# Layer norms and half of the kept-edge evictions of batches 1 to 3: from ACT to DVE, in a quantile-aggregation graph layer

## The chip, the core and the metric

The kernel runs on one core of a Trainium2 chip. The metric is device time in microseconds (us) of one execution, lower being better. A core has a matrix engine (PE), a vector engine (DVE), an activation engine (ACT), GpSimd (POOL) and a synchronisation engine (SP) whose queue issues most plain DMAs here. Each works through its own list of instructions in order; they meet through semaphores.

## The reference

The input is `x` (16 batches of 1024 nodes, 64 values each), a symmetric 0/1 adjacency `adj` (16 x 1024 x 1024, about 8 neighbours a node, with self loops) and a mask that is all ones. Cut to what matters:

```python
h = jnp.maximum(_layernorm(x, axis=-1), 0.0)
# inside the layer, on h, with T, K = 10, 2:
neigh = (adj_ > 0) & ~eye
rank  = jnp.cumsum(ni, axis=-1) - ni            # place of an edge in its row
skip  = jnp.where(nb > T, (nb + K - 1) // K, 1) # nb: neighbours of the node
rem   = neigh & (sk > 1) & (rank % sk == sk - 1) & mask[:, :, None]
rem   = rem | jnp.swapaxes(rem, 1, 2)
nd    = jnp.where(rem, 0.0, adj_) > 0           # edges that are kept
# quantiles 0.25, 0.5, 0.75 of h over the kept neighbours, weighted 0.25, 0.5, 0.25
agg   = sum of w * (v_lo + frac * (v_hi - v_lo))
out   = h + agg
y     = relu(out @ W1 + b1) @ W2 + b2
return x + y * mask
```

So rows with more than 10 neighbours drop a few edges; for each node and each of 64 channels the values at the remaining neighbours are sorted, and three quantiles of them are added to the node's own value before a small two-layer perceptron.

## The kernel before, in words

A batch passes through these stages, each a generator (a Python function that emits instructions and yields) inside `list_layer`:

- `load(b)` (L892): eight adjacency tiles of 128 rows come in by SP's DMAs (`ask`, L813, two buffers). ACT makes 0/1 values of each (L904), PE transposes them (L911), and ACT writes the result as fp8 (L924). `number` (L934) counts the neighbours; its counts go to `cnt`.
- `drop(b)` (L970): PE computes ranks into PSUM, ACT takes a distance (L991), DVE marks dropped edges in `rem` (L992).
- `normalize(b)` (L1198): the layer norm and ReLU. SP loads `x` of the batch into `xt` (L1200, a single buffer). For batch 0 DVE does it in eight whole-tile instructions around one square root on ACT (L1205 to L1213). For the others `scaled` (L1177) does it on ACT in pieces of 64 columns: eight sums (L1181) and eight sums of squares (L1186), each of them two instructions since the accumulator is read out, then eight normalised ReLUs (L1194). L1219 and L1220 copy the values into `pack`; L1231 stores `h` to a table in DRAM, from which the gathers read.
- `keep(b)` (L995): PE subtracts dropped edges in both directions in two PSUM halves for each of eight tiles (L1004 to L1009). The halves are clamped at zero and written to `kept` as fp8: by ACT (L1014), except that for batch 0 DVE writes the second half of each tile (L1012). PE then makes bit codes of the kept edges (L1017), ACT copies them to `pack` (L1022).
- `order(b)` (L1025): nodes are ranked by their number of edges, and DVE builds a permutation matrix `perm` (L1063). `rem` and `perm` share one buffer (the tag "wide"), so `drop` of the next batch can only begin to write when this batch's `perm` has been read.
- `collect(b)` (L1067): PE permutes codes and values (L1088), ACT copies out the values (L1093 to L1098), DVE extracts the neighbour indices (L1103 to L1132). The last of them, L1132, writes the index list `idx`. With it the batch's gathers can begin.

`prepare(b)` (L1629) emits `drop(b)`, `load(b+1)` and `normalize(b)` interleaved, then `keep`, `order` and `collect`.

Batches are used in pairs. `fetch(m)` (L1253) queues the gathers of pair m: 63 for each batch, in four classes of node tiles, all of them indirect DMAs issued by POOL (L1265). The buffers of the first two classes are double, those of the last two single. `aggregate` (L1350) sorts the gathered values with compare-exchange networks of DVE minimum and maximum (L1300, L1305), weighs them (L1316), sums them on PE (L1320); `mlp` (L1448) ends the work on a batch. The main loop (L1678) weaves aggregation and perceptron of pair m-1 with the preparation of pair m+1.

The order in which each engine runs its instructions is not that of emission. `arrange` (L641) takes all instructions with their dependences, prices each (`Step.cost`, L614), and simulates a list schedule: an engine that is free takes, among the instructions that are ready in the model, the one that was emitted first. The resulting sequence of each engine is then fixed by added dependences. On the chip an engine that meets an instruction whose data is not there waits, even if a later one could run.

In `keep` and `normalize` the choice of the engine is made by the batch number; these are the conditions that the change touches:

```python
if b == 0 and n:          # keep, L1011: second half of each tile
    nc.vector.tensor_scalar(kept[:, 4:], kp, 0.0, None, OP.max, saturate=False)
...
if b == 0:                # normalize, L1203
```

Of the kernel before, what the change touches and what calls it, by code (L numbers as in the profile page):

```python
# [547 lines left out]
            main(b, iter(()))  # L548


ENGINES = ("PE", "ACT", "DVE", "POOL", "SP")
NAMES = {"PE": "PE", "DVE": "DVE", "Activation": "ACT", "Pool": "POOL", "SP": "SP"}

# [87 lines left out]
def arrange(tc, runs, loose, tails):  # L641
# [59 lines left out]

    free, wire = dict.fromkeys(ENGINES, 0.0), 0.0
    waiting, able, sequence = ({e: [] for e in ENGINES} for _ in range(3))
# [49 lines left out]
def list_layer(  # L753
# [138 lines left out]
    def load(b, fast=False):  # L892

        ne = wk.tile([P, NT, N], FP8, name="ne", bufs=2)
        neT[b] = ne
        nbs[b] = [wk.tile([P, NT], F32, name=n) for n in ("bias", "half")]
        for t in range(NT):
            ask(b, t)
            at = asked.pop((b, t))
            sg = wk.tile([P, N], BF16, name="sg")  # L900
            if fast and t % 2:
                nc.gpsimd.tensor_scalar(sg, at, 0.0, None, OP.is_gt)
            else:
                nc.scalar.activation(sg, at, AF.Sign)  # L904
            ask(*divmod(b * NT + t + 2, NT))
            for n in range(2):
                tp = psum.tile([P, 4, P], F32, name="tp", tag="mx", bufs=3)
                run = []
                for s in range(4):
                    m = 4 * n + s  # L910
                    run.append(nc.tensor.matmul(  # L911
                        tp[:, s], sg[:, m * P:(m + 1) * P], ident16, start=(s == 0), stop=(s == 3 and t // 4 != n),
                        skip_group_check=True,
                    ))
                if t // 4 == n:
                    run.append(
                        nc.tensor.matmul(tp[:, t % 4], minus16, ident16, start=False, stop=True, skip_group_check=True)  # L917
                    )
                settle(run)
                to = ne[:, 4 * n:4 * n + 4, t * P:(t + 1) * P]  # L920
                if fast and n:
                    nc.vector.tensor_scalar(to, tp, 0.0, None, OP.max, saturate=False)
                else:
                    nc.scalar.activation(to, tp, AF.Relu, saturate=False)  # L924
            if fast and t == 3:
                number(b, 0, 4)
            yield 0.1
        if fast:
            number(b, 4, NT)
        else:  # L930
            number(b, 0, NT)
        yield 1.4

    def number(b, lo, hi):  # L934

        ne = neT[b]
        bias, half = (k[:, lo:hi] for k in nbs[b])
        for n in range(lo // 4, hi // 4):
            cols = slice(n * HALF, (n + 1) * HALF)

            cp = psum.tile([P, HALF], F32, name="cp", tag="mx", bufs=3)
            run = []
            for k in range(2):
                for q in range(4):
                    run.append(nc.tensor.matmul(
                        cp[32 * q:32 * q + 32], one[:, 1 - k:33 - k], ne[:, 2 * q + k, cols], start=(k == 0),
                        stop=(k == 1), skip_group_check=True,
                    ))
            settle(run)
            if b == 0 and n:  # L950
                nc.vector.tensor_copy(cnt[:, cols], cp)
            else:
                nc.scalar.copy(cnt[:, cols], cp)
        nb = psum.tile([P, NT], F32, name="nb", tag="misc")
        settle([
            nc.tensor.matmul(nb[:, t:t + 1], cnt[:, t * P:(t + 1) * P], ones16[:, 0:1], start=True, stop=True)
            for t in range(lo, hi)
        ])
        nb = nb[:, lo:hi]

        sk = wk.tile([P, NT], I32, name="sk")[:, lo:hi]
        nc.vector.tensor_scalar(sk, nb, 1.0, None, OP.add)
        many = wk.tile([P, NT], F32, name="many")[:, lo:hi]
        nc.vector.scalar_tensor_tensor(many, nb, 10.0, mask[:, b, lo:hi], OP.is_gt, OP.mult)
        nc.vector.tensor_scalar(sk, sk, 1, None, OP.logical_shift_right)
        nc.vector.tensor_scalar(bias, sk, -1.5, -2047.0, OP.mult, OP.add)
        nc.vector.tensor_scalar(half, sk, 0.5, 1.0, OP.mult, OP.add)
        nc.vector.tensor_tensor(half, half, many, OP.mult)
# [26 lines left out]
    def keep(b):  # L995

        ne, rem = neT.pop(b), rems.pop(b)
        for t in range(NT):
            ts = slice(t * P, (t + 1) * P)
            kept = wk.tile([P, NT, P], FP8, name="kept")  # L1000
            for n in range(2):
                kp = psum.tile([P, 4, P], F32, name="kp", tag="mx", bufs=3)
                run = [
                    nc.tensor.matmul(kp, plus, ne[:, 4 * n:4 * n + 4, ts], start=True, stop=False),  # L1004
                    nc.tensor.matmul(kp, minus, rem[:, 4 * n:4 * n + 4, ts], start=False, stop=False),  # L1005
                ]
                for s in range(4):
                    at = (4 * n + s) * P
                    run.append(nc.tensor.matmul(kp[:, s], rem[:, t, at:at + P], minus, start=False, stop=(s == 3)))  # L1009
                settle(run)  # L1010
                if b == 0 and n:  # L1011
                    nc.vector.tensor_scalar(kept[:, 4:], kp, 0.0, None, OP.max, saturate=False)  # L1012
                else:
                    nc.scalar.activation(kept[:, 4 * n:4 * n + 4], kp, AF.Relu, saturate=False)  # L1014
            code = psum.tile([P, NT, 17], F32, name="code", tag="code", bufs=2)
            settle([
                nc.tensor.matmul(  # L1017
                    code[:, s], kept[:, s], octet, start=(s == 0), stop=(s == NT - 1), skip_group_check=True
                )
                for s in range(NT)  # L1020
            ])
            nc.scalar.copy(pack[:, t, :KEYS], code.rearrange("p s k -> p (s k)"))  # L1022
            yield 0.1
# [174 lines left out]
    def normalize(b):  # L1198
        xt = wk.tile([P, NT, C], F32, name="xt", bufs=1)
        nc.sync.dma_start(out=xt, in_=x[b].rearrange("(t p) c -> p t c", p=P))  # L1200
        h = xt
        mean, var = (wk.tile([P, NT], F32, name=n) for n in ("mean", "var"))
        if b == 0:  # L1203
            shape, square = [P, NT, C], wk.tile([P, NT, C], F32, name="square", tag="highs", bufs=1)
            nc.vector.tensor_reduce(mean, xt, AX.X, OP.add)  # L1205
            nc.vector.tensor_scalar(mean, mean, -1.0 / C, None, OP.mult)
            nc.vector.tensor_tensor(h, xt, mean[:, :, None].to_broadcast(shape), OP.add)
            nc.vector.tensor_tensor(square, h, h, OP.mult)
            nc.vector.tensor_reduce(var, square, AX.X, OP.add)
            nc.scalar.activation(var, var, AF.Sqrt, bias=eps, scale=1.0 / C)  # L1210
            nc.vector.reciprocal(var, var)
            nc.vector.tensor_tensor(h, h, var[:, :, None].to_broadcast(shape), OP.mult)
            nc.vector.tensor_scalar(h, h, 0.0, None, OP.max)  # L1213
            yield 0.4
        else:
            yield from scaled(xt, mean, var)

        halves, bytes_ = (h.rearrange("p t c -> p (t c)").bitcast(d).rearrange("p (t c k) -> p t c k", t=NT, c=C) for d in (BF16, U8))
        nc.scalar.copy(pack[:, :, VALUES:VALUES + C], halves[:, :, :, 1])  # L1219
        nc.scalar.copy(  # L1220
            pack[:, :, VALUES + C:].rearrange("p t (c k) -> p t c k", k=2), bytes_[:, :, :, 0:2]
        )
        nc.scalar.copy(pack[:, :, OWN + 2], mask[:, b])
        grp, at = divmod(b, GROUP)
        for g in range(B // GROUP) if b == 0 else ():
            group_tab[g] = dram.tile([GROUP, FRONT + N, C], F32, name="gtab", bufs=B // GROUP)
            nc.sync.dma_start(
                out=group_tab[g][:, 0:FRONT].rearrange("b n c -> b (n c)").rearrange("b (s k) -> b s k", s=SLICE),
                in_=none,
            )  # L1230
        nc.sync.dma_start(out=group_tab[grp][at, FRONT:].rearrange("(t p) c -> p t c", p=P), in_=h)  # L1231
        tables[b] = group_tab[grp].rearrange("b n c -> (b n) c")[:(at + 1) * (FRONT + N)], at * (FRONT + N) * C
        yield 0.1
# [641 lines left out]
```

## Time and profile before

| | |
|---|---|
| median of 3 runs | 1548.63 us (1544.91 to 1550.77) |
| the profiled execution | 1547.62 us |
| its span, first to last instruction | 1545.8 us |
| instructions | 28097 |
| mean granted PE clock | 0.84 of full speed |
| ACT busy | 915.4 us (59%) |
| gathers on POOL | 1008, mean 1.05 us each |
| index lists ready (L1132), batches 0 to 5 | 68.4 and 77.2 (two parts), 149.1, 210.8, 273.8, 343.4, 401.7 us |
| first and last gather begin | 68.9 and 1487.5 us |

The profile is one execution. An engine's busy share is an average over stages that have different limits; what ended each idle time, and when, is read from the timeline. A record's duration runs from its start to its end in the engine's pipeline, and records of one engine overlap, so that a sum of durations can be larger than the time that the engine needed. In groups, the columns are: line, engine, operation, tiles, shapes, count, then busy us and mean ns of one, then idle time before them and what ended it.

### The profile page before, as it was taken

The page shows a single profiled execution, that of the slowest core. Times are in us where ns is not written, and L with a number is a line of the kernel's source. Part 1 is how long each engine was busy: PE and PEld are TensorE (multiplying, and loading weights), DVE is VectorE, ACT ScalarE, POOL GpSimd, SP SyncE. Part 2 cuts the span into 40 slices and gives each one's busy share as a digit, 9 for nine tenths or more (in the row PEclk, how much of TensorE's full clock was granted, in tenths as well). Part 3 has the DMA queues.
Part 4 walks back from the last instruction along what each step waited for, and adds up shares of the span by engine and source line. Part 5 has one row for each costly group of instructions (what it writes and reads, how often), then busy time and mean ns, then how long its engine had stood idle before and what let it go on. Part 6 is the DMA issues. An engine that isn't in the chain of part 4 may idle for free.

```text
span 1545.8 us, 28097 instructions
## 1 busy us (share of the span) xinstructions
PE 1067.7 (69%) x8411; PEld 663.0 (43%) x8411; DVE 1249.8 (81%) x6125; ACT 915.4 (59%) x2504; POOL 1110.3 (72%) x1051
## 2 busy tenths in 40 slices
PE   6777867889886986798829964459867942450256
PEld 3444544555564544455516543335534521220223
DVE  5625389985899889978996798988998899689784
ACT  6998976989877884789557682186834410110001
POOL 3177775777777777777777777777777777777760
PEclk9979869899998998899869996769977975685567
DMA  6353432434433343335322342232311121121100
GB/s 213 103 178 87 118 93 78 114 86 122 96 111 86 88 126 83 87 76 129 85 66 79 67 133 50 45 100 59 93 34 28 26 53 24 30 52 24 25 15 16
DMA packets 128532, 122.85 MB, mean 79 GB/s; under 512 B 94546, under 2 KB 95090, under 8 KB 128370
## 3 DMA queue, kind: packets, MB, share of 16 engines
q1 hardware_dynamic: 95026, 86.77, 18.6%
q0 software_dynamic: 33344, 34.19, 12.0%
q8 instruction: 68, 1.11, 0.3%
q14 instruction: 94, 0.77, 0.2%
HBM read 110.10 MB, written 9.05 MB: 77 GB/s over the span
## 4 chain that ended last, share of the span: by engine, by line
ACT 28%; PE 23%; issue 18%; POOL 14%; DVE 10%; DMA 6%; DVEq 0%; SPq 0%; ACTq 0%; POOLq 0%
POOL g L1265 13%; PE codeP L1088 6%; ACT dist L991 5%; PE acc L1320 5%; ACT sg L904 4%; ACT ne L924 3%; ACT kept L1014 3%; DVE g L1300 2%; ACT waste L1186 2%; DMA at<-in_adj_dram 2%; DMA g<-gtab,idx 2%; DVE g L1305 2%; ACT waste L1181 2%; ACT xt L1194 2%; PE rk L981 1%
## 5 line engine op out<-in xcount | busy, mean ns | idle before, releaser
L1265 POOL DMA_INDIRECT g<-gtab,idx x1008 | 1055.0, 1047 | 367.7 <-issue 288.6
L1305 DVE TENSOR_TENSOR g<-g 128x384 f32<-128x384 f32 (+2 forms) x675 | 310.7, 481 | 6.4 <-DMA gg<-g 6.1
L1300 DVE TENSOR_TENSOR g<-g 128x384 f32<-128x384 f32 (+2 forms) x675 | 313.2, 484 | 1.5
L1320 PE MATMUL acc<-g,kf 128*128 128x128 f32 (+2 forms) x472 | 141.0, 448 | 159.9 <-DVE g L1316 106.6
L1088 PE MATMUL codeP<-pack,perm 128*128 128x332 bf16 x1024 | 184.9, 321 | 14.9 <-DVE perm L1063 14.5
L991 ACT ACTIVATE dist<-rk,bias 128x512 f16<-128x512 f32 x256 | 168.5, 708 | 31.2 <-DVE rem L992 19.9
L981 PE MATMUL rk<-kb,cnt 128*128 128x512 bf16 x256 | 112.5, 440 | 91.4 <-ACT dist L991 85.5
L1320 PEld LDWEIGHTS acc<-g,kf 128*128 128x128 f32 x472 | 90.1, 232 | 188.5 <-DVE g L1316 110.6
L911 PE MATMUL tp<-kb,sg 128*128 128x128 bf16 x1024 | 108.2, 242 | 71.6 <-ACT sg L904 50.2
L1014 ACT ACTIVATE kept<-kp 128x512 fp8e4<-128x512 f32 x248 | 146.8, 615 | 11.3 <-PE kp L1009 9.3
L924 ACT ACTIVATE ne<-tp 128x512 fp8e4<-128x512 f32 x248 | 141.5, 622 | 17.1 <-PE tp L917 9.7
L986 PEld LDWEIGHTS <-ne 128*128 128x128 fp8e4 x1024 | 89.9, 109 | 143.8 <-issue 120.9
L799 DVE MEMSET pause<- 128x1 bf16 x2340 | 138.1, 59 | 0.0
L904 ACT ACTIVATE sg<-at 128x1024 bf16<-128x1024 f32 x121 | 128.7, 1086 | 5.2 <-DMA at<-in_adj_dram 5.2
L1088 PEld LDWEIGHTS <-perm 128*128 128x128 bf16 x1024 | 93.4, 101 | 78.2 <-DVE perm L1063 37.8
L911 PEld LDWEIGHTS <-sg 128*128 128x128 bf16 x1024 | 80.6, 109 | 95.3 <-ACT sg L904 56.0
L986 PE MATMUL rk<-kw,ne 128*128 128x128 fp8e5 x1024 | 118.3, 241 | 0.0
L992 DVE TENSOR_SCALAR rem<-dist,half 128x1024 bf16<-128x1024 f16 x128 | 64.2, 503 | 52.2 <-ACT dist L991 51.4
L1009 PE MATMUL kp<-kw,rem 128*128 128x128 fp8e5 x1024 | 99.4, 218 | 0.0
L1004 PE MATMUL kp<-ne,kw 128*128 128x512 fp8e4 x256 | 97.2, 380 | 0.4 <-ACT dist L991 0.2
L1005 PE MATMUL kp<-rem,kw 128*128 128x512 bf16 x256 | 96.5, 377 | 0.0
L1418 DVE TENSOR_SCALAR at_p<-iota,node 128x512 bf16<-128x512 f16 x256 | 85.6, 376 | 11.8 <-PE low L1440 11.8
(189 smaller groups left out, 2071.5 us busy)
## 6 DMA issues: line engine op xcount, KB each, us to landing
at<-in_adj_dram SPq DMA_DIRECT2D x122, 512.0 KB
g<-gtab,idx POOLq DMA_INDIRECT x1008
xt<-in_x_dram SPq DMA_DIRECT2D x16, 256.0 KB
y<-in_x_dram SPq DMA_DIRECT2D x16, 256.0 KB
gtab<-xt SPq DMA_DIRECT2D x16, 256.0 KB
out_dram<-y SPq DMA_DIRECT2D x14, 256.0 KB
spare<-in_adj_dram SPq DMA_DIRECT2D x6, 512.0 KB
gg<-g SPq DMA_DIRECT2D x32, 48.0 KB
```

What stands on the lines that cost most here:

```text
L799: tails[nc.vector.memset(pause[:, at:at + 1], 0.0).ins.name] = ins.ins.name
L904: nc.scalar.activation(sg, at, AF.Sign)
L911: run.append(nc.tensor.matmul(tp[:, s], sg[:, m * P:(m + 1) * P], ident16, start=(s == 0), stop=(s == 3 and t // 4 != n), skip_group_check ...
L924: nc.scalar.activation(to, tp, AF.Relu, saturate=False)
L986: run.append(nc.tensor.matmul(rk[:, s * P:(s + 1) * P], ne[:, 4 * n + s, ts], upper, start=False, stop=(s == 3), skip_group_check=True,))
L991: nc.scalar.activation(dist[:, n * HALF:(n + 1) * HALF], rk, AF.Abs, bias=bias[:, t:t + 1])
L1014: nc.scalar.activation(kept[:, 4 * n:4 * n + 4], kp, AF.Relu, saturate=False)
L1088: run.append(nc.tensor.matmul(flat, perm[:, t, k * P:(k + 1) * P], pack[:, t], start=False, stop=(t == NT - 1), skip_group_check=True,))
L1265: return nc.gpsimd.indirect_dma_start(out=gathered[m, tiles][:, slot, k - lo, h], out_offset=None, in_=tables[2 * m + h][0], in_offset=bas ...
L1300: nc.vector.tensor_tensor(at(f + k * df, df, many), pa, pb, OP.min if what == "<" else OP.max)
L1305: nc.vector.tensor_tensor(pa if back else pb, pa, pb, OP.max if what == "<" else OP.min)
L1320: nc.tensor.matmul(acc, ident32, lines[:, s], start=False, stop=(s == now[-1] and not ends), skip_group_check=True)
```

## The change

Three constants take the place of the tests for batch 0. Batches 1 to 3 now take the path of batch 0 in `normalize` (DVE, L1205 to L1213) and in `keep` (DVE evicts the second half of each tile, L1012). With `LOADB = 0` the tests in `load` and `number` select what they selected before. Batches 4 to 15 stay on ACT for both. Since `arrange` sees other instructions, the sequence of every engine is made anew.

```diff
+LOADB, KEEPB, NORMB = 0, 3, 3
 ENGINES = ("PE", "ACT", "DVE", "POOL", "SP")
...
                 to = ne[:, 4 * n:4 * n + 4, t * P:(t + 1) * P]
-                if fast and n:
+                if b <= LOADB and n:
                     nc.vector.tensor_scalar(to, tp, 0.0, None, OP.max, saturate=False)
...
             settle(run)
-            if b == 0 and n:
+            if b <= LOADB and n:
                 nc.vector.tensor_copy(cnt[:, cols], cp)
...
                 settle(run)
-                if b == 0 and n:
+                if b <= KEEPB and n:
                     nc.vector.tensor_scalar(kept[:, 4:], kp, 0.0, None, OP.max, saturate=False)
...
         mean, var = (wk.tile([P, NT], F32, name=n) for n in ("mean", "var"))
-        if b == 0:
+        if b <= NORMB:
             shape, square = [P, NT, C], wk.tile([P, NT, C], F32, name="square", tag="highs", bufs=1)
             nc.vector.tensor_reduce(mean, xt, AX.X, OP.add)
```

## The prediction

> **What bounds the kernel now.** I read the page first (busy shares, slices, costliest groups), then POOL's timeline, since POOL has the one digit that never changes, then the instructions that POOL waited for, then ACT's and DVE's load stage by stage.
>
> ```profile
> PE 1067.7 (69%) x8411; PEld 663.0 (43%) x8411; DVE 1249.8 (81%) x6125; ACT 915.4 (59%) x2504; POOL 1110.3 (72%) x1051
> POOL 3177775777777777777777777777777777777760
> L1265 POOL DMA_INDIRECT g<-gtab,idx x1008 | 1055.0, 1047 | 367.7 <-issue 288.6
> ```
>
> POOL is busy 72% by the page, and yet it is the bound. Each of its 1008 gathers takes about 1.05 us and is followed by 0.3 us marked "issue" (288.6 us in 947 times), in which it waits for nothing. A 7 in a slice thus means back to back. Its timeline, where the last number is the idle time before an instruction and what ended it:
>
> ```profile
> 68.89 1.17 POOL L1265 DMA_INDIRECT g<-gtab,idx  x1 [47.01 <-DVE idx L1132]
> ...
> 149.65 0.95 POOL L1265 DMA_INDIRECT g<-gtab,idx  x1 [0.70 <-DVE idx L1132]
> ...
> 259.61 1.02 POOL L1265 DMA_INDIRECT g<-gtab,idx  x1 [0.30 <-issue]
> 274.34 0.95 POOL L1265 DMA_INDIRECT g<-gtab,idx  x1 [13.71 <-DVE idx L1132]
> ...
> 1487.50 0.95 POOL L1265 DMA_INDIRECT g<-gtab,idx  x1 [0.30 <-issue]
> ```
>
> The first gather waits for the index list of batch 0, gather 64 for that of batch 1, and gather 148, after a hole of 13.71 us, for that of batch 3. From 274.34 to 1488.4 no idle time over 0.30 us is left, but for about 2 us around the two scatters at 1121. The rest is a tail of 57.4 us behind the last gather. So the time is: first gather 68.9, gathers back to back, one hole of 13.4 us (13.71 less the usual 0.30), and the tail. The page's chain of waits gives ACT 28% and POOL only 14%: followed back through the short idle times it steps onto other engines at chance meetings, which is why I trust POOL's own timeline here.
>
> When do the lists come? DVE's timeline has one L1132 for each list:
>
> ```profile
> 149.12 0.26 DVE L1132 SCALAR_TENSOR_TENSOR idx<-bit,low 128x104 int32<-128x104 f32 x1
> 210.84 0.32 DVE L1132 SCALAR_TENSOR_TENSOR idx<-bit,low 128x104 int32<-128x104 f32 x1
> 273.81 0.26 DVE L1132 SCALAR_TENSOR_TENSOR idx<-bit,low 128x104 int32<-128x104 f32 x1
> ```
>
> One list in about 62 us, against 63 gathers of a batch in 81 to 83. POOL reaches batch 3 at 260.6 and its list at 274. Batch 4's list (343.4) is used only at about 413 and batch 5's (401.7) at about 430, so nothing later is short by less than 25 us.
>
> What paces the lists? The busy time of each engine by stage (PE, PEld, DVE, ACT, POOL):
>
> ```profile
> 40.00:180.00 140.00, 110.47 (x1090) 69.92 (x1087) 56.44 (x270) 130.10 (x367) 84.50 (x87) 0.89 0.44 124
> 180.00:280.00 100.00, 71.33 (x599) 44.58 (x598) 90.47 (x458) 72.71 (x215) 66.78 (x66) 0.82 0.31 82
> ```
>
> From 40 to 180 us ACT is full (93%) and DVE 40% busy; from 180 to 280 it is the other way round. The change moves work from ACT to DVE in just these stages: good in the first, doubtful in the second.
>
> [...] gathers come every 1.28 us while DVE is 44% busy (gathers 1 to 63; DVE from 60 to 160) and every 1.36 while it is 87% busy (274 to 1487, 892 POOL instructions), a weak dependence. [...]
>
> **The change part by part.** The first two hunks change nothing: the flag is set for batch 0 alone.
>
> Layer norms, batches 1 to 3. Off ACT, per batch (means from the groups of 0 to 330 us): 8 x (0.282+0.217) + 0.217 + 8 x (0.375+0.218) + 8 x 0.459 = 12.6 us; the square root stays. These records overlap: start to start they are 0.38, 0.47 and 0.37 us apart, so ACT's time is nearer 9.9. Onto DVE, by batch 0's instructions: 0.68+0.17+0.69+0.69+0.68+0.20+0.69+0.43 = 4.2, less the 0.36 of L1190 and L1191 that go: 3.9 us. Kept edges: per batch 8 of 16 evictions leave ACT at 0.615 (4.9 us) and come to DVE at 0.69 (5.5 us). Sum over three batches: 53 us of ACT records off, 28 us of DVE on.
>
> What that is worth on the path to batch 3's list:
> - Batch 0. Its norm is on DVE already, but batch 1's norm sits on ACT from 45.5 us among batch 0's kept edges. DVE's half of them came 1.56 us apart (41.99, 43.55, 45.10, 46.66), and then 2.40 and 2.04:
>
> ```profile
> 45.10 0.69 DVE L1012 TENSOR_SCALAR kept<-kp 128x512 fp8e4<-128x512 f32 x1 [0.87 <-ACT pack L1022]
> 46.66 0.69 DVE L1012 TENSOR_SCALAR kept<-kp 128x512 fp8e4<-128x512 f32 x1 [0.86 <-ACT waste L1181]
> 49.06 0.69 DVE L1012 TENSOR_SCALAR kept<-kp 128x512 fp8e4<-128x512 f32 x1 [1.71 <-ACT waste L1181]
> 51.10 0.69 DVE L1012 TENSOR_SCALAR kept<-kp 128x512 fp8e4<-128x512 f32 x1 [1.34 <-PE kp L1009]
> ```
>
>   Behind ACT's waste and square instructions two tiles lose 1.3 us, and L1194 stands among batch 0's collect from 64.4: up to 3 us for the first gather. But 4.2 us of DVE come into the same gaps. I take 1.5; bounds -1 and +3.
> - Batch 1. Its drop (L991 from 81.9) waits for its load and numbering to end (81.2), in a stretch where ACT is full and holds 9.9 us of norm. The drop cannot begin before batch 0's permutation is read (71.7, one buffer for both). I take 9 us. Its kept edges (108.3 to 122.8, 14.6 us) hold half of batch 2's norm; with that gone and DVE taking half, PE is next: at batch 0's 1.56 a tile 12.5 us remain. Another 2.
> - Batches 2 and 3. The drops (142 to 163, 209 to 228) are ACT with the next load, and keep their length but for 4 waste pairs at 147.4: 1 us. Kept edges 2 us each. The serial order and collect (some 30 us) stay. So 3 for batch 2 and, with no waste pairs, 2 for batch 3.
> - Against that: DVE now waits in order for the x transfer of batches 2 and 3, issued at 82.1 and 144.4; behind it stand the last list steps and the next drop's L992. ACT's own such wait was 2.93 us (at 207.65). Between 0 and 3 each; I take 0.5.
>
> The list of batch 3 comes 1.5+9+2+3+2-1 = 16.5 us earlier, at 257.3. Bounds: 9 (only ACT's start-to-start time of one norm counts) and 25. POOL would get there at 260.6-1.5-0.4 = 258.7. But POOL's order is static, made by the planner from modelled times: gather 148 is batch 3's first, after only 9 of batch 2's 27 of the second class, as the planner expected the list then. With less ACT work it will expect it earlier, by up to 9 gathers. Since it prices the norm's ACT instructions low (no accumulator read of 0.2 us), its shift is less than the real one; I take 3 gathers, 3.9 us, which leaves a hole of about 2.5.
>
> Store of h and load of the next x: L1231 and L1200 go with the norm through SP's queue, between adjacency loads; they come earlier, and h is read by gathers 25 us later at the soonest. L1219 and L1220 stay on ACT behind collect. The square's buffer is shared with mlp's, first used after 340. Neither costs.
>
> POOL: 28 us more DVE beside it, 4 of them before its first gather. By the two rates above, 0.08 us a gather for 43 points of load, that is 28/1.36 x 0.19 = 4 us at most[...].
>
> Sum: hole 13.4-2.5 = 10.9, first gather 1.5, hole at gather 64 0.4, POOL -1.0: 11.8 us. The profiled execution took 1547.62 (span 1545.8, 1.8 around it): 1535.8. The median shown is 1.0 above it: 1537.
>
> After 274 everything moves with POOL. What is late next: pair 1's last two classes need pair 0's buffers (begin copies at 323.6, gather 205 at 351.2), 27 us of slack. DVE is 87% busy from 280 to 1488 and keeps up.
>
> **The rivals.** (A, 0.52) As above, 1537, own range 1531 to 1541. (B, 0.16) Half of it: the list gains only 9 us, or the planner puts batch 3 at gather 139 and POOL waits there; 13.4 shrinks by 4 to 6 and the rest is eaten: 1544. For: the order is made from a model. (C, 0.17) Slower: DVE becomes the pacer of the list. In 200 to 260 it is 18 to 20 of 20 busy with sorts beside batch 3; if batch 3's keep still falls there (231 to 245), its evictions and the 5.5+3.9 us stand in that line, and the hole grows by 9.4 less 1.5: 1548.6+7.9 = 1556.5. It decides from the point where batch 3's keep begins after about 225 and the sorts stand ahead. Against: sorts come later in program order, which is the planner's priority, and the norm falls before 190 where DVE is idle. (D, 0.15) More: no hole left and 2.5 at the first gather: 1531 to 1533.
>
> **How the numbers follow.** No change is what a measurement of this kernel cannot tell from it, within 0.5% (7.7 us). Faster: A 0.50, D 0.15, B 0.03: 0.68. Same: B 0.13, A 0.02: 0.15. Slower: C, 0.17. The range holds A, B and D, and the first-gather bounds: 1529 to 1548.
>
> **What would show it.** Right: the list of batch 3 before 262; a hole of 0 to 5 us at batch 3's first gather; ACT below 80% and DVE near 60% in 40 to 180; the same tail of 57 us. Wrong: list 3 at 270 or later; DVE instructions as the releaser of the kept evictions after 225; a new hole over 2 us after 280, or gathers slower than 1.37 us.

## The result, and the profile after

| | before | after |
|---|---|---|
| median | 1548.84 us (9 runs, 1544.72 to 1550.77) | 1539.56 us (9 runs, 1534.6 to 1541.8) |
| the profiled execution | 1547.62 (span 1545.8) | 1541.8 (span 1540.1) |

The ratio of the times is 0.9941 with a 95% interval of 0.9927 to 0.9954: 9.3 us faster. 1537 had been forecast, in a range of 1529 to 1548. The number came out, but the path to it did not: the profile after shows a different account. Seven of the twelve experiments ran on chips where the kernel before also took 2714 to 2744 us, some 1.77 times as long; they are told of together and used for little.

The page after, its line of busy times, POOL's slices and POOL's costliest group:

```profile
PE 1065.0 (69%) x8411; PEld 668.5 (43%) x8411; DVE 1271.1 (83%) x6167; ACT 882.1 (57%) x2357; POOL 1091.9 (71%) x1051
POOL 3177776777777777777777777777777777777720
L1266 POOL DMA_INDIRECT g<-gtab,idx x1008 | 1042.7, 1034 | 363.3 <-issue 286.2
```

ACT lost 33 us of busy time and DVE gained 21. POOL's last slice went from 6 to 2: its gathers end earlier, and something else ends the kernel. (All line numbers after are one higher: the gather L1265 is L1266 here.) POOL's timeline after, the columns being start, duration, engine, instruction and in brackets the idle time ahead with its releaser:

```profile
68.99 1.17 POOL L1266 DMA_INDIRECT g<-gtab,idx  x1 [46.65 <-DVE idx L1133]
...
149.90 1.23 POOL L1266 DMA_INDIRECT g<-gtab,idx  x1 [0.30 <-DVE xt L1208]
...
261.91 0.94 POOL L1266 DMA_INDIRECT g<-gtab,idx  x1 [0.30 <-issue]
272.97 0.94 POOL L1266 DMA_INDIRECT g<-gtab,idx  x1 [10.12 <-DVE idx L1133]
...
1471.79 1.13 POOL L1266 DMA_INDIRECT g<-gtab,idx  x1 [0.30 <-issue]
```

The first gather did not move (68.89 before). The hole ahead of batch 3's gathers shrank from 13.71 to 10.12 us, no more. The last gather starts 15.7 us earlier, yet the span is only 5.7 us shorter: from the end of the last gather to the end of the kernel 57.4 us went by before (1488.45 to 1545.8), and 67.2 go by now (1472.9 to 1540.1). The lists on DVE, which were at 149.12, 210.84 and 273.81:

```profile
147.09 0.26 DVE L1133 SCALAR_TENSOR_TENSOR idx<-bit,low 128x104 int32<-128x104 f32 x1
206.02 0.32 DVE L1133 SCALAR_TENSOR_TENSOR idx<-bit,low 128x104 int32<-128x104 f32 x1
272.44 0.26 DVE L1133 SCALAR_TENSOR_TENSOR idx<-bit,low 128x104 int32<-128x104 f32 x1
```

They are 2.0, 4.8 and 1.4 us earlier. The load by stage (busy us of PE, PEld, DVE, ACT, POOL), in the stretches shown of before:

```profile
40.00:180.00 140.00, 112.36 (x1129) 74.67 (x1129) 81.47 (x327) 109.43 (x254) 84.80 (x87) 0.89 0.44 126
180.00:280.00 100.00, 69.53 (x565) 42.55 (x564) 92.03 (x454) 65.94 (x200) 69.77 (x68) 0.83 0.33 90
```

In 40 to 180 us ACT fell from 130.1 to 109.4 (78%) and DVE rose from 56.4 to 81.5 (58%), just as forecast. From 40 to 280 DVE has 26.6 us more to do, close to the 28 counted, and it fell behind in nothing: of its compare-exchange instructions (L1300 and L1305, one line higher after) 189 had started by 380 us in both, and 297 before and 305 after by 480 us. The new work went into idle DVE time.

What ends the kernel, if not POOL? What DVE waited for from 1440 us to the end of the kernel after (total us, times, longest):

```profile
DVE highs L1462 <- PE low L1441: 7.0, 1, 7.0
DVE highs L1462 <- ACT highs L1461: 5.3, 3, 3.6
DVE yp L1509 <- PE yp L1505: 3.0, 3, 2.4
DVE few L1593 <- ACT o L1591: 2.3, 1, 2.3
```

This is the whole list, and no gather is in it. Nor is one in DVE's list from 280 to 1440 us, before or after; ACT waited for gathers twice in that stretch after the change (20.9 and 9.0 us) and PE once (3.4). DVE's last sorts that wait for gathers start here, before and after:

```profile
1515.51 0.42 DVE L1300 TENSOR_TENSOR g<-g 128x256 f32<-128x256 f32 x1
```

```profile
1509.86 0.42 DVE L1301 TENSOR_TENSOR g<-g 128x256 f32<-128x256 f32 x1
```

That is 27 us after the end of the last gather before the change, and 37 us after it now. A mark on DVE's timeline instead of POOL's gives a tail of constant length. The first line here is of the kernel before, the second of the kernel after:

```profile
1443.44 0.30 DVE L1508 TENSOR_TENSOR yp<-yp,gapart 128x128 f32<-128x128 f32 x1 [10.34 <-PE yp L1504]
```

```profile
1438.06 0.30 DVE L1509 TENSOR_TENSOR yp<-yp,gapart 128x128 f32<-128x128 f32 x1 [9.94 <-PE yp L1505]
```

From this instruction to the end it is 102.4 us before and 102.0 after, though the last gather comes 44 us behind it in the one and 34 in the other. By these two traces the end was set before 1440 us, on the side that uses the gathered data, while POOL ran ahead of it. So the forecast's frame, POOL's gathers back to back with a fixed tail, was in doubt, and the experiments began there.

### The profile page after: what moved, and what is told of

Same layout as the page of the kernel before. It is cut to its first block, busy times and chain, and to the rows that moved or that the text cites. A ratio compares the mean times of both kernels' runs of the same rounds, so it can differ in the third digit from the quotient of the medians.

```text
span 1540.1 us, 28016 instructions
## 1 busy us (share of the span) xinstructions
PE 1065.0 (69%) x8411; PEld 668.5 (43%) x8411; DVE 1271.1 (83%) x6167; ACT 882.1 (57%) x2357; POOL 1091.9 (71%) x1051
## 4 chain that ended last, share of the span: by engine, by line
PE 21%; issue 18%; ACT 15%; POOL 14%; DVE 11%; DMA 5%; DVEq 0%; SPq 0%; POOLq 0%; ACTq 0%
POOL g L1266 14%; PE codeP L1089 5%; PE acc L1321 5%; DMA g<-gtab,idx 3%; ACT dist L992 3%; DVE g L1301 2%; DVE g L1306 2%; ACT sg L905 2%; ACT ne L925 2%; ACT kept L1015 2%; PE high L1435 1%; DVE gg L1301 1%; ACT waste L1182 1%; DMA xt<-in_x_dram 1%; PE low L1441 1%
## 5 line engine op out<-in xcount | busy, mean ns | idle before, releaser
L1266 POOL DMA_INDIRECT g<-gtab,idx x1008 | 1042.7, 1034 | 363.3 <-issue 286.2
L1301 DVE TENSOR_TENSOR g<-g 128x256 f32<-128x256 f32 (+2 forms) x675 | 313.2, 485 | 1.6 <-PE acc L1365 0.6
L1306 DVE TENSOR_TENSOR g<-g 128x256 f32<-128x256 f32 (+2 forms) x675 | 312.2, 484 | 2.2 <-PE acc L1365 1.9
L1321 PE MATMUL acc<-g,kf 128*128 128x128 f32 (+2 forms) x472 | 146.2, 455 | 198.2 <-DVE g L1317 101.6
L1089 PE MATMUL codeP<-pack,perm 128*128 128x332 bf16 x1024 | 181.5, 317 | 6.6 <-DVE perm L1064 5.9
L992 ACT ACTIVATE dist<-rk,bias 128x512 f16<-128x512 f32 x256 | 168.5, 698 | 22.9 <-PE rk L987 8.7
L925 ACT ACTIVATE ne<-tp 128x512 fp8e4<-128x512 f32 x248 | 138.9, 609 | 16.0 <-PE tp L918 10.5
L1015 ACT ACTIVATE kept<-kp 128x512 fp8e4<-128x512 f32 x224 | 133.6, 613 | 22.5 <-ACT pack L1023 10.5
L993 DVE TENSOR_SCALAR rem<-dist,half 128x1024 bf16<-128x1024 f16 x128 | 64.7, 507 | 56.0 <-ACT dist L992 54.8
L1094 ACT CAST st<-codeP 128x4 bf16<-128x4 f32 x128 | 21.4, 167 | 138.9 <-PE codeP L1089 138.2
```

Source lines behind the costliest of these rows:

```text
L992: nc.scalar.activation(dist[:, n * HALF:(n + 1) * HALF], rk, AF.Abs, bias=bias[:, t:t + 1])
L1089: run.append(nc.tensor.matmul(flat, perm[:, t, k * P:(k + 1) * P], pack[:, t], start=False, stop=(t == NT - 1), skip_group_check=True,))
L1266: return nc.gpsimd.indirect_dma_start(out=gathered[m, tiles][:, slot, k - lo, h], out_offset=None, in_=tables[2 * m + h][0], in_offset=bas ...
L1301: nc.vector.tensor_tensor(at(f + k * df, df, many), pa, pb, OP.min if what == "<" else OP.max)
L1306: nc.vector.tensor_tensor(pa if back else pb, pa, pb, OP.max if what == "<" else OP.min)
L1321: nc.tensor.matmul(acc, ident32, lines[:, s], start=False, stop=(s == now[-1] and not ends), skip_group_check=True)
```

## The experiments

Theory P is that of the forecast: POOL paces the kernel, and its hole is worth its length. Theory D: the sorts and what is done beside them on DVE pace it, and POOL follows. What five other kernels gave, beside before and after, on chips of the usual speed; the hole is the idle time ahead of batch 3's first gather less the usual 0.30 us, "list 7" is the index list of batch 7 (those of batches 8 to 15 follow, up to 1237.7 us before and 1233.1 after), "mark" is the DVE instruction of the last fence. A ratio is against executions of the kernel before on the same chip as the row's own (median 1548.19 us for the four rows that fill the hole or take one part, 1547.26 for the last), and it is not the quotient of the two medians. The columns after the ratio are from one profiled execution each, and such an execution may lie 4 us from its kernel's median.

| kernel | median | ratio to before | list 3 | hole | list 7 | mark | last gather | span |
|---|---|---|---|---|---|---|---|---|
| before | 1548.84 | | 273.81 | 13.4 | 547.91 | 1443.44 | 1487.50 | 1545.8 |
| before, hole filled | 1546.93 | 0.9985 (0.9974 to 0.9996) | 273.38 | 0 | 544.53 | 1439.48 | 1470.37 | 1541.5 |
| after | 1539.56 | 0.9941 (0.9927 to 0.9954) | 272.44 | 9.8 | 539.60 | 1438.06 | 1471.79 | 1540.1 |
| after, hole filled | 1539.82 | 0.9925 (0.9901 to 0.9949) | 269.31 | 0 | 537.12 | 1436.93 | 1465.86 | 1539.1 |
| norms alone | 1546.33 | 0.9983 (0.9973 to 0.9994) | 272.16 | 10.5 | 543.67 | 1445.09 | 1477.36 | 1547.2 |
| kept edges alone | 1549.88 | 1.0009 (0.9995 to 1.0024) | 278.11 | 14.6 | 549.63 | 1443.59 | 1476.88 | 1546.9 |
| after, with 14 reductions | 1537.11 | 0.9940 (0.9925 to 0.9955) | 268.40 | 9.4 | 535.94 | 1430.54 | 1472.79 | 1533.7 |

### The hole filled, without and with the change

For pair 1 alone, the gathers of both classes of batch 2 are queued ahead of batch 3's, so that POOL has work while it would wait for batch 3's list. No engine gets more or less work, but the order of every engine is planned anew; the first run is made from the kernel before, the second from the kernel after.

```diff
-            fetch(m, CLASSES[:1])
+            fetch(m, CLASSES[:1]) if m > 1 else fetch(m, CLASSES[:2], halves=(0,))
...
-            fetch(m, CLASSES[1:2])
+            fetch(m, CLASSES[1:2]) if m > 1 else fetch(m, CLASSES[:2], halves=(1,))
```

> The kernel before, with one thing changed: for pair 1 all first- and second-class gathers of batch 2 are queued ahead of batch 3's, so that POOL has 39 gathers of work instead of 21 before it needs batch 3's list. No engine gets more or less work. Theory P (POOL's gathers and the tail behind the last one set the end): the hole of 13.4 us goes, last gather about 1474, time about 1535, ratio 0.991. Theory D (from about 190 us on DVE's own line sets the end and POOL runs ahead of it): the hole goes and the last gather comes about 13 us earlier too, but the tail behind it grows by as much; time 1546 to 1551, ratio 0.998 to 1.002.

> The changed kernel with the same reordering of pair 1's gathers. Theory P: its remaining hole of 9.8 us goes, time about 1530, ratio to before 0.988. Theory D: the gathers end about 10 us earlier and the time stays at 1537 to 1541, ratio 0.993 to 0.996.

POOL's timeline of the kernel before with the hole filled, around the place where the hole was, and its last gather:

```profile
259.13 1.04 POOL L1265 DMA_INDIRECT g<-gtab,idx  x1 [0.30 <-issue]
...
263.14 0.94 POOL L1265 DMA_INDIRECT g<-gtab,idx  x1 [0.30 <-issue]
...
1470.37 1.14 POOL L1265 DMA_INDIRECT g<-gtab,idx  x1 [0.31 <-issue]
```

In the kernel before POOL stood for 13.71 us at gather 148 with 18 gathers of batch 2 behind it, whose list was there at 210.84. With these ahead of it the hole is gone, and the last gather is 17 us earlier than before, earlier even than in the kernel after. It would be earlier still, but at 1107 us POOL now waits for a result of the other side, the store of `y`, where before no idle time in that place was over 0.63 us:

```profile
1107.25 1.09 POOL L1597 DMA_INDIRECT out_dram<-gx,gto  x1 [11.68 <-DMA out_dram<-y]
```

The time moved by 0.15%, about 2 us. In the kernel after, filling the hole brought the last gather 6 us forward and the median not at all (1539.82 against 1539.56). Theory P is refuted: the gathers' end can be moved by 17 us with next to nothing for the time.

### Each part alone

Norms alone has the layer norms on DVE and leaves the kept edges on ACT; kept edges alone is the reverse.

```diff
-LOADB, KEEPB, NORMB = 0, 3, 3
+LOADB, KEEPB, NORMB = 0, 0, 3
```

```diff
-LOADB, KEEPB, NORMB = 0, 3, 3
+LOADB, KEEPB, NORMB = 0, 3, 0
```

> The norms of batches 1 to 3 on DVE, kept edges as before. Theory D: the gain comes from DVE work done while DVE is idle (40 to 180 us) and from ACT's relief bringing DVE's other work forward; the norms free the most of ACT (38 of 53 us of records), so most of the gain: time about 1542, ratio 0.995 to 0.997. Theory P: the list of batch 3 comes some 1 to 2 us earlier, hole about 12, time 1546 to 1548.

> Half of the kept edges of batches 1 to 3 on DVE, norms as before. Theory D: 16.6 us of DVE work more, partly in idle time, and shorter keep stages (2 us each for batches 1 and 2): time 1543 to 1550, ratio 0.997 to 1.001. Theory P: the list of batch 3 some 2 to 4 us earlier, so 1545 to 1547.

The norms alone gain 0.17%, the kept edges alone nothing that can be told from zero, and both together 0.59%. The parts do not add up. For the norms alone theory D missed (0.995 to 0.997 expected) and theory P's 1546 to 1548 came out; for the kept edges alone theory D's range holds the result, and theory P's earlier list did not come (278.11). The trace of kept edges alone suggests why it gains nothing. ACT's timeline among batch 1's kept edges:

```profile
113.69 0.58 ACT L1015 ACTIVATE kept<-kp 128x512 fp8e4<-128x512 f32 x1
114.16 0.26 ACT L1023 CAST pack<-code 128x136 bf16<-128x136 f32 x1
114.31 0.27 ACT L1182 ACTIVATE waste<-xt 128x64 f32<-128x64 f32 x1
...
115.46 0.26 ACT L1182 ACTIVATE waste<-xt 128x64 f32<-128x64 f32 x1
115.63 0.19 ACT L1182 ACTIVATION_READ_ACCUMULATOR waste<-xt 128x1 f32 x1
115.72 0.58 ACT L1015 ACTIVATE kept<-kp 128x512 fp8e4<-128x512 f32 x1
```

The evictions that left ACT made room, and the planner, which sets the order of the instructions from modelled durations, put more of the next norm into it: here four sums (L1182, each with its accumulator read), and from 109 to 124 us eight sums, eight sums of squares and five normalised pieces, where before there were eight sums and four sums of squares. DVE's half of the same edges then still comes every 1.55 to 2.2 us:

```profile
117.92 0.69 DVE L1013 TENSOR_SCALAR kept<-kp 128x512 fp8e4<-128x512 f32 x1 [1.31 <-PE kp L1010]
120.08 0.69 DVE L1013 TENSOR_SCALAR kept<-kp 128x512 fp8e4<-128x512 f32 x1 [1.48 <-PE kp L1010]
```

The stage took 13.7 us from the first to the last pack copy, against 12.4 before; with the norm gone too, 10.6 us. In the kernel after, the same instructions in batch 1:

```profile
114.35 0.69 DVE L1013 TENSOR_SCALAR kept<-kp 128x512 fp8e4<-128x512 f32 x1 [0.88 <-ACT pack L1023]
115.90 0.69 DVE L1013 TENSOR_SCALAR kept<-kp 128x512 fp8e4<-128x512 f32 x1 [0.86 <-ACT pack L1023]
117.46 0.69 DVE L1013 TENSOR_SCALAR kept<-kp 128x512 fp8e4<-128x512 f32 x1 [0.87 <-ACT pack L1023]
```

One every 1.55 us, batch 0's pace. But norms alone reaches 10.6 us in this stage as well, with the kept edges still on ACT. So the length of this stage is owed to the norm's leaving, which is a likely account of why kept edges alone gain nothing; it does not account for the other half, that both together gain 0.42% more than the norms alone. That stays open. In the table norms alone has list 7 at 543.67 and both at 539.60, which places the difference ahead of 540 us, though from single executions.

### More work on DVE

If DVE paces the kernel, added DVE work must cost its length. Fourteen reductions were added to the kernel after, two in each of pairs 0 to 6; the results are used by nothing.

```diff
+                if m < 7:
+                    nc.vector.tensor_reduce(busy, iota, AX.X, OP.max)
                 terms(acc, [
```

It ran three times, twice on the 1.77x chips and once on a usual one:

> The changed kernel with one idle reduction of 128x1024 (about 1.1 us) on DVE after each half of pairs 0 to 6: 14 x 1.13 = 16 us more for DVE, its result unused. Theory D: most of it shows: 1551 to 1556, ratio 1.001 to 1.005. Theory P: no change, 1537 to 1543.

> The same kernel as e6 (16 us more for DVE after the halves of pairs 0 to 6), which had run on a chip where every kernel took 1.77 times its usual time. Theory D: 1551 to 1556, ratio to before 1.001 to 1.005. Theory P: 1537 to 1543, ratio 0.992 to 0.996.

> The same kernel as e6 and e10 (16 us more for DVE), whose two calls both met chips on which every kernel took 1.77 times its usual time. If the kernel before runs at about 1548: theory D 1551 to 1556, ratio 1.001 to 1.005; theory P 1537 to 1543, ratio 0.992 to 0.996.

On the usual chip: 0.9940, where the kernel after has 0.9941. That is no verdict on theory D, as the view of these instructions by tile shows (durations in ns least/median/greatest, then the first and last start in us):

```profile
L1408 DVE TENSOR_REDUCE busy<-iota x14: 1168/1210/1220, 3.0 to 38.8; 128x1 f32<-128x1024 f16 x14
```

They took 1.21 us each by the median, where 1.13 had been expected. They read a constant and depend on nothing else, so the planner put all 14 (16.9 us) into the first 39 us; in the kernel after DVE is busy for 20.7 of the first 40. The run shows two other things: these 16.9 us of DVE work before 40 us cost nothing that can be seen, and a third order of the program with both parts of the change in it has the same gain, so that the gain does not hang on one order.

A mended version reduces the pair's own output, so that it can't run early.

```diff
                 ])
+                if m < 7:
+                    nc.vector.tensor_reduce(busy, o[:, 4 * half:4 * half + 4], AX.X, OP.max)
```

> The changed kernel with a reduction of each half's 128x1536 results on DVE (about 1.74 us each, by 1.21 us for 1024 elements), result unused, for pairs 0 to 6: 14 x 1.74 = 24 us more for DVE that cannot run before its half is aggregated, unlike the reductions of e6, e10 and e11, which depended on nothing and ran in the first 40 us. Theory D (DVE's line sets the end from about 190 us on): 15 to 24 us slower than the changed kernel, 1554 to 1564, ratio to before 1.004 to 1.010. If DVE's remaining idle time (about 183 us after 280) can take work without cost: 1537 to 1542, ratio 0.993 to 0.996. On a chip that runs everything at 1.77 times, the same difference is to be read against e6 and e10.

```profile
L1411 DVE TENSOR_REDUCE busy<-o x14: 1734/1748/1754, 535.8 to 2455.9; 128x8 f32<-128x1536 bf16 x14
```

By the same view these 24.5 us do lie among the sorts now. But the run fell on a 1.77x chip: 2703.9 us, a ratio of 0.9949 (0.9933 to 0.9964), not slower than the early reductions there (0.9964 and 0.9970). Its page says why this settles nothing for the usual chip:

```profile
PE 1155.9 (43%) x8411; PEld 709.1 (26%) x8411; DVE 1291.8 (48%) x6181; ACT 892.5 (33%) x2357; POOL 1011.8 (37%) x1051
```

No engine is above half busy there, where DVE on the usual chip is at 83%. What late DVE work costs on a usual chip stays open, and theory D with it.

### The other runs on the 1.77x chips

Twelve gathers done twice, in pairs 2 to 5, some 16 us of POOL at the usual pace, added to the kernel after (run twice):

```diff
+            for k in tiles if lo == 1 and 2 <= m <= 5 else ():
+                queue.append(partial(gather, 0, order[0], k, PASSED[k]))
```

> The changed kernel with 12 gathers done twice (pairs 2 to 5, three each, same source and target): 12 x 1.34 = 16 us more for POOL, nothing for the others. Theory P: 1555, ratio 1.004. Theory D: the last gather comes about 16 us later, into a slack of about 27 us between it and the sort that needs it; time 1537 to 1543, ratio 0.992 to 0.996.

> The same kernel as e5 (12 gathers done twice, 16 us more for POOL), since that call ran at 1.77 times the usual times for every kernel and left the question open. Theory P: 1555, ratio to before 1.004. Theory D: 1537 to 1543, ratio 0.992 to 0.996, with the last gather about 16 us later than in the changed kernel.

All norms on DVE, and the kept edges of batch 5 as well:

```diff
-LOADB, KEEPB, NORMB = 0, 3, 3
+LOADB, KEEPB, NORMB = 0, 3, 15
```

```diff
-                if b <= KEEPB and n:
+                if (b <= KEEPB or b == 5) and n:
```

> The norms of all 16 batches on DVE, kept edges as in the changed kernel. 12 x 3.9 = 46 us more for DVE, nearly all in stages where it is the fuller engine. Theory D: slower than the changed kernel by 20 to 46 us, the less where DVE's waits for ACT get shorter; ratio to before 1.008 to 1.025. Theory P: same as the changed kernel or faster.

> The changed kernel with half of batch 5's kept edges on DVE too: they fall in 340 to 380 us, where ACT is full and DVE idle for 16 of 40 us. Theory D: 5.5 us of DVE work go into idle time, as in 40 to 180 us, so 1534 to 1540, ratio 0.990 to 0.995. Theory P: no effect, 0.994.

| kernel | median | before, same chips | ratio |
|---|---|---|---|
| gathers twice | 2755.71 | 2739.17 | 1.0065 (1.0042 to 1.0089) |
| gathers twice, again | 2732.13 | 2714.57 | 1.0073 (1.0056 to 1.0090) |
| early reductions | 2728.94 | 2739.17 | 0.9964 (0.9953 to 0.9975) |
| early reductions, again | 2736.07 | 2743.94 | 0.9970 (0.9959 to 0.9982) |
| all norms on DVE | 2716.94 | 2739.17 | 0.9929 (0.9908 to 0.9950) |
| kept edges of 1, 2, 3 and 5 | 2726.57 | 2739.17 | 0.9959 (0.9946 to 0.9971) |

There the doubled gathers cost about 1% against the kernels with reductions and come near theory P's 1.004, and with more DVE work no kernel was slower than the kernel before (0.9929 with all norms on DVE, 0.9959 to 0.9970 with the others), the reverse of what theory D expects of it (1.008 to 1.025 for all norms). But POOL was not short of time there. In the second run with doubled gathers it waited 675 us for PE:

```profile
POOL g L1266 <- PE acc L1323: 674.7, 10, 123.4
```

A gather done twice may also hold up the sort that reads it, which was not tested; the kernel after itself was not run on these chips; and runs from chips like that of the page above, with DVE at 48%, can't be carried over to a chip where it is 83% busy. In a profile of these chips ACT's timeline has idle times such as this one (gathers twice, second run), whose releaser, "remote", names no instruction of the kernel:

```profile
153.98 0.69 ACT L992 ACTIVATE dist<-rk,bias 128x512 f16<-128x512 f32 x1 [10.52 <-remote]
```

No version was found that is shown to beat the kernel after: filling its hole gave an interval of 0.9901 to 0.9949 that covers the kernel after, and all norms on DVE was not run on a usual chip.

## Why the prediction was right, and where it was wrong

The time of 1537 lay 2.6 us from the median, and the sign was right. Of the signs that the prediction had named, the load by stage came out, and no new hole or slower gather appeared; but list 3 came after 270, a hole of 9.8 us was left, and the tail was 67 us and not 57. The steps:

- **"So the time is: first gather 68.9, gathers back to back, one hole of 13.4 us ..., and the tail."** This is the step that failed. Each number in it was right, and the sum gave the span, as any cut of a span into stretches does. The error was to take the tail of 57.4 us as constant. With the hole filled the tail is 70 us; over the seven kernels of the table it runs from 57 to 72. The stretch from the mark on DVE to the end has 102.0 to 103.3 us in all seven. POOL is back to back, with 0.30 us between two gathers, because the next gather's list and buffer are there in time; that anyone waits for the one in hand does not follow from it, and DVE, which sorts the data, did not in the traces before and after. The page's chain of waits, which gave POOL 14%, had been set aside.
- **"I take 9 us"** for batch 1's drop measured nothing: its first L993 starts at 83.19, before (L992) at 83.24. ACT was full there (busy for 29.9 of the 31 us from 52 to 83), but not only of the norm: it runs in its planned order, and its own inputs hold it. ACT's timeline after:

```profile
57.60 1.06 ACT L905 ACTIVATE sg<-at 128x1024 bf16<-128x1024 f32 x1 [0.20 <-DMA at<-in_adj_dram]
59.80 1.06 ACT L905 ACTIVATE sg<-at 128x1024 bf16<-128x1024 f32 x1 [1.15 <-DMA at<-in_adj_dram]
66.51 0.16 ACT L1094 CAST st<-codeP 128x4 bf16<-128x4 f32 x1 [1.16 <-PE codeP L1089]
71.63 0.16 ACT L1094 CAST st<-codeP 128x4 bf16<-128x4 f32 x1 [0.74 <-PE codeP L1089]
72.32 1.56 ACT L925 ACTIVATE ne<-tp 128x512 fp8e4<-128x512 f32 x3
```

  The adjacency's DMA and batch 0's collect through PE (3.8 us of waits in six places) release it, and the load's last tiles start at 72.32, against 72.36 before (L924). The freed 20.7 us of ACT became idle time.
- **"Another 2" for batch 1's kept edges and 2 for those of batches 2 and 3.** Measured 1.8 (12.4 to 10.6 us), 1.2 (11.9 to 10.7) and nothing (12.1 to 12.2). PE's pace of 1.56 us a tile, taken from batch 0, was right for the first two (1.52). In batch 3 DVE's evictions came 1.6 to 2.2 us apart, 1.9 in the mean, with sorts beside them. That fits the mechanism of rival C, at the place it named, too small to decide.
- **The list of batch 3 "comes ... 16.5 us earlier, at 257.3"** came 1.4 us earlier, at 272.44, and the planner moved gather 148 by one place the other way, not by three: batch 3's first is now gather 149. The hole gave 3.6 us of the 10.9 forecast.
- **First gather, 1.5:** measured −0.1. Batch 0's norm was on DVE already, and the list behind its collect did not move.
- **"POOL: ... -1.0", a cost,** had the wrong sign: from 275 us to the last gather the mean fell from 1055 to 1039 ns over some 860 gathers. The change need not have done it: the kernel before with its hole filled has no engine work changed and shows 1037 over nearly the same stretch. To take 1 us of the "4 us at most" was the author's estimate, shown by no run; and the two rates behind the 4 us, 1.28 and 1.36 us a gather, are of two stages that differ in more than DVE's load (DMA share 0.46 and 0.30). No slowing is to be seen. And the idle times at the two scatters at 1121 were 0.30 and 0.63 us, not about 2.
- **Instruction counts and durations held:** DVE's new norm instructions took 680, 166, 693, 690, 684, 195, 688 and 426 ns, 4.2 us as counted from batch 0's; a kept eviction took 691 ns; the busy times by stage came out as said. "Everything moves with POOL" after 274 did not.

Why then 9.3 us, near the 11.8 summed? In the forecast they were the hole. The traces allow another account, made afterwards. DVE's busy time up to 280 us and from there to the end, before and after (length, then busy us, then clock, DMA share and GB/s):

```profile
0.00:280.00 280.00, 167.61 (x791) 0.87 0.42 121
280.00:1545.80 1265.80, 1082.18 (x5334) 0.83 0.29 70
```

```profile
0.00:280.00 280.00, 194.17 (x843) 0.88 0.43 125
280.00:1540.10 1260.10, 1076.90 (x5324) 0.83 0.28 70
```

By 280 us DVE had done 26.6 us more, but only 21.3 of them are added work; 5.3 us less was left to it, its idle time after 280 us stayed as it was, and the span is 5.7 us shorter. The same for all seven kernels of the table:

| kernel | DVE busy after 280 us | DVE idle after 280 us | span |
|---|---|---|---|
| before | 1082.2 | 183.6 | 1545.8 |
| before, hole filled | 1079.6 | 181.9 | 1541.5 |
| after | 1076.9 | 183.2 | 1540.1 |
| after, hole filled | 1075.3 | 183.8 | 1539.1 |
| norms alone | 1074.4 | 192.8 | 1547.2 |
| kept edges alone | 1083.3 | 183.6 | 1546.9 |
| after, with 14 reductions | 1072.9 | 180.8 | 1533.7 |

In six of them the idle time is 181 to 184 us, whatever POOL does, and the span follows the work left to DVE within 3 us. Kept edges alone leave as much as before. Norms alone leave as little as both parts, but idle 9.6 us longer than the kernel after, 9.4 of them in 280 to 380 and 480 to 580 us; why, these runs do not show. Nor can the gain be followed list by list: list 7 is 8.3 us earlier, the lists of batches 10 and 11 are 4.7 and 5.3 us later than before, and the last one, of batch 15, is 4.6 us earlier. This speaks for theory D, but it compares single executions and is not a cause shown by changing it alone: why the idle time is the same in six orders, and what work added late to DVE costs on a usual chip, stays open. That the number agreed is chance: a gain counted where it was not, and another, of like size, not foreseen.

## What to carry to other kernels

That an engine runs back to back does not make it the bound, as POOL shows here (last gather 17 us earlier, time 0.15% shorter): look in the waits of its consumers, and measure the tail from more than one engine before calling it constant; filling the hole with other work of that engine is a cheap test. Time freed on an engine that runs in a fixed order need not be time gained for the next stage, as ACT's 20.7 us show: see what released its instructions there, a DMA or another engine, and what the planner puts into the room. Count for the engine suspected instead how much work is left to it at some point, and how long it idles after. And parts of a change tested one by one need not add up: here −0.17% and +0.09% made −0.59%.

## What was not expected of the hardware

The mean duration of the indirect DMA's issue on POOL differs between kernels with no cause found in them: 1055, 1039 and 1037 ns in nearly the same stretch of the kernels before, after and before with the hole filled, 14 to 16 us over some 860 gathers, though the first and the last have the same instructions on every engine. Each mean is from one execution, so that what belongs to the kernel and what to the execution can't be told apart. POOL's groups in that stretch, of the kernel before and of the kernel before with the hole filled (count, then busy us and mean ns, then idle us and its releasers):

```profile
L1265 POOL DMA_INDIRECT g<-gtab,idx x861 | 908.2, 1055 | 275.8 <-issue 248.4 <-DVE idx L1132 13.7 <-DMA g<-gtab,idx 7.3
```

```profile
L1265 POOL DMA_INDIRECT g<-gtab,idx x859 | 890.7, 1037 | 261.8 <-issue 246.9 <-DMA g<-gtab,idx 7.9 <-DVE pause L799 0.9
```

The other surprise was the chips on which every kernel takes some 1.77 times as long (the kernel before 2714 to 2744 us, against 1548.84): in one of their profiles, of the kernel after with late reductions, DVE's busy time less the 24.5 us of the reductions and ACT's are about those of the kernel after on a usual chip (1267.3 and 892.5 us against 1271.1 and 882.1), POOL's is shorter (1011.8 against 1091.9), PE's longer (1155.9 against 1065.0), and the mean granted PE clock is 0.69 against 0.84. What is added is idle time, the span being 2707.0 us against 1540.1; at some places it is tens of us with "issue" or "remote" as its end, in the first run with early reductions up to 31.9 us ahead of a weight load of PE ("issue") and up to 32.6 ahead of ACT's L925 ("remote"). Its cause stays open.
